# Attention in a four-layer graph network: scores turned so that the keys lie on the partitions, a multiplied mask instead of an added one, no maximum, and the old network kept behind a branch

## The chip, the cores and the metric

The kernel runs on one core of a Trainium2 chip. A core has five engines that work side by side: TensorE (PE; its loads of weights are listed as PEld), VectorE (DVE), ScalarE (ACT), GpSimd (POOL) and SyncE (SP, which issues transfers). The metric is the device time of one execution in microseconds, the median of several runs.

## The reference

There are 128 graphs of 64 nodes with 256 features. Four layers follow each other, each with a layer norm and a ReLU ahead of it and a residual sum after it. The change concerns the first two, which are attention layers with 8 heads of 32 features:

```python
# layer 0 (biases bq, bk, bv, bo)
scores = jnp.einsum('bhqd,bhkd->bhqk', q, k) / np.float32(np.sqrt(HD))
scores = jnp.where(adj[:, None, :, :] > 0, scores, jnp.float32(NEG))      # NEG = -9e15
attn = jax.nn.softmax(scores, axis=-1)
out = jnp.einsum('bhqk,bhkd->bhqd', attn, v)
return out.transpose(0, 2, 1, 3).reshape(b, n, D_OUT) @ Wo + bo
# layer 1 (only bo)
scores = jnp.einsum('bhqd,bhkd->bhqk', q, k) / math.sqrt(HEAD_DIM)
scores = scores + jnp.log(adjacency + 1e-06)[:, None, :, :]
attn = jax.nn.softmax(scores, axis=-1)
# ... the same as above
```

Layer 2 is a gated graph network of five steps (a product with the adjacency, then a GRU cell with two sets of 256x768 weights); layer 3 mixes a normalized graph convolution with a plain product by a gate. All is in fp32. Every node has an edge to itself, so no row of the adjacency is empty.

## The kernel before

Two graphs share the 128 partitions (a pair); four pairs make a group, and there are 16 groups. Python records every operation with an estimated cost, and a planner (`Plan.run`) then emits them in an order that mixes the attention of one group with the GRU of another and the last layer of a third. Small matmuls use parts of the array: the planner knows the modes T64 (tiles of 64x64: scores and aggregation), T32 (64 rows by 32 columns: the weighting of the values) and TURN (transpositions). PSUM is two sets of four banks, of which attention and the last layer share the tag "a" and the GRU's sums have the tag "g".

The attention of two pairs, one "step" (16 groups x 2 layers x 2 halves = 64 steps):

```python
# [cut: layer norm, projections q, k, v]
pss = [bank(f"s_{name}_{i}") for i in range(2)]

def scores():
    for i in range(2):                      # which graph of a pair
        for c in range(2):                  # which half of the heads
            for gp in range(2):             # which pair
                for rh in range(2):
                    # [cut: s, t0]
                    ps = pss[rh].tile.rearrange("p (h i k) -> p h i k", h=4, i=2)
                    nc.tensor.matmul(ps[gp * NODES : (gp + 1) * NODES, 2 * c : 2 * c + 2, i, :],
                                     qk[s, c, gp, 0, i * NODES : (i + 1) * NODES],
                                     k_exp[s, c, :, t0 : t0 + NODES], start=True, stop=True)
# [cut: the last step's weigh() is put ahead of scores(), its finish() behind]
for i in range(2):
    ps, e = pss[i], es[i]
    vec(dve(512), ... scalar_tensor_tensor(e, ps, scale, bias_at(pp) ..., op0=mult, op1=add))
    vec(dve(512), ... tensor_reduce(m, e8(), axis=X, op=max))
    vec2(dve(512), ... tensor_tensor(e8(), e8(), m ..., op=subtract))
    sca(act(512, 0.5), ... activation(e, e, AF.Exp))
    vec(dve(512), ... tensor_reduce(z, e8(), axis=X, op=add))
    vec(109, ... reciprocal(z, z))
    pool(1000, ... gpsimd.tensor_tensor(e8(), e8(), z ..., op=mult))
    pa = bank(f"aT_{name}_{i}")
    pe(437, turn, ...)                      # four 128x128 transpositions of e into pa
    sca(act(512), ... activation(aT, pa, AF.Copy))

po = [bank(f"o_{name}_{i}") for i in range(2)]

def weigh():
    for gp in range(2):
        s = slice(gp * NODES, (gp + 1) * NODES)
        for c in range(2):
            for q in range(4):
                for i in range(2):
                    rows, h = slice(i * NODES, (i + 1) * NODES), 4 * c + q
                    o = po[i][:, :D].rearrange("p (c t) -> p c t", c=2)
                    nc.tensor.matmul(o[q * HD : (q + 1) * HD, c, s], v[rows, gp, h * HD : (h + 1) * HD],
                                     aTs[q // 2][rows, 2 * c + q % 2, s], start=True, stop=True)

def finish():
    for i in range(2):
        vec(dve(256), ... tensor_copy(oT[:, i], po[i][:, :D] ...))
    # [cut: four 256-column matmuls of oT with w_o into py]
    vec(dve(512), ... tensor_tensor(xt, py, xt, op=add))
```

(Calls are shortened with "..."; the cost in front is the planner's, in ns.) For each group the mask is made ready once: `neg` is NEG where the adjacency is zero, on VectorE; `ladj = Ln(adj + 1e-6)` on ScalarE, once for two groups.

Of the kernel before, what the change touches and what calls it, by code (L numbers as in the profile page):

```python
# [11 lines left out]
ALU = mybir.AluOpType  # L12
# [62 lines left out]
FUSE = -1.1  # L75
FUSE_SPAN = 0.25


# [190 lines left out]


@with_exitstack
def gnn_stack_kernel(ctx: ExitStack, tc: tile.TileContext, a: dict, out: bass.AP):
    nc = tc.nc
    x, adj, nodemask = a["x"], a["adj"], a["nodemask"]
    n_pairs = x.shape[0] // 2
# [94 lines left out]
    with plan.strand(-3.0, 0.1):  # L370


        few = new("few", [P, 7 + PAIRS], 1)

# [4 lines left out]
        fill(slice(1, 1 + PAIRS), 1, -0.5)  # L379
        parity, k_bias = PAIRS + 1, PAIRS + 3  # L380
        fill(slice(parity, parity + 2), 2, 0.0)
        for q in range(4):
            fill(slice(parity + q % 2, parity + q % 2 + 1), 2, 1.0, slice(q * HD, (q + 1) * HD))
        ident = new("ident", [P, P], 1)
        pool(600, lambda: make_identity(nc, ident.tile), [], [ident])
# [13 lines left out]
        def fill_rows():  # L399
            r0 = 0  # L400
            for name in ("L0_gnn_bq", "L0_gnn_bk", "L2_gnn_b_ih", "L2_gnn_b_hh", "L0_gnn_bv"):
                n = a[name].shape[0] // P
                nc.scalar.dma_start(rows.tile[r0 : r0 + n, :], a[name].rearrange("(r p) -> r p", p=P))
                r0 += n
            nc.scalar.dma_start(rows.tile[r0 : r0 + n_pairs, :],
                                nodemask.rearrange("(t a) n -> t (a n)", a=2))
# [6 lines left out]
        def load_first(layer, i):  # L413
            t, j = (first[layer], i) if i < 2 else (first[2], layer)
            dma(256, lambda: nc.sync.dma_start(
                t[:, j], a[f"L{layer}_gnn_W{'qkv'[i]}"].rearrange("(c p) o -> p c o", p=P)), [], [(t, j)])
            return t, j
# [48 lines left out]
    with plan.strand(-0.9, 0.1):  # L466

        w_o, bo = attn[0]
        bvb = new("aT", [P, 4, P], 2, "bvb")
        pbo = bank("bvo")  # L470
        for c in range(2):
            vec(200, lambda c=c: nc.vector.tensor_copy(
                bvb[:, c, :], cols[:, 16 + c : 17 + c].to_broadcast([P, P])), [cols], [(bvb, c)])
            pe(mm(256), lambda c=c, w_o=w_o: nc.tensor.matmul(
                pbo[:, :D], bvb[:, c, :], w_o[:, c, :], start=c == 0, stop=c == 1),
                [(bvb, c), w_o], [pbo])
        vec(dve(256), lambda bo=bo: nc.vector.tensor_tensor(bo.tile, pbo[:, :D], bo.tile, op=ALU.add),
            [pbo, bo], [bo])
# [25 lines left out]
    def power(dst, src, at, eps, n, name):  # L504

        s = new("pw", [P, n], 3, f"pw_{name}")
        vec2(70, lambda: nc.vector.tensor_scalar(s.tile, at(), eps, None, op0=ALU.add), [src], [s])  # L507
        pool(660 if n == 2 else 970, lambda: nc.gpsimd.tensor_tensor(dst.tile, s.tile, few[:, 1 : 1 + n], op=ALU.pow),  # L508
             [s, (few, 1)], [dst], port=2)
# [24 lines left out]

    def norm_relu_t(xt, half, dst, access, writes, name, by_token=None, by_graph=False):

        st = new("st", [P, 2, 6], 3, f"st_{name}")
        mv = new("mv", [P, 2, 2], 3, f"mv_{name}")
        rstd = new("rstd", [P, 2], 3, f"rstd_{name}")
        for i in range(2):  # L540
            p = 2 * half + i
            vec(332, lambda p=p, i=i: nc.vector.bn_stats(st[:, i, :], xt[:, p, :]), [(xt, p)], [(st, i)])
            vec(83, lambda i=i: nc.vector.bn_aggr(mv[:, i, :], st[:, i, :]), [(st, i)], [(mv, i)])
        power(rstd, mv, lambda: mv[:, :, 1], EPS, 2, name)
        xn = new("xn", [P, 2, D], 1, f"xn_{name}")
        for i in range(2):
            p = 2 * half + i
            vec2(325, lambda p=p, i=i: nc.vector.tensor_scalar(
                xn[:, i, :], xt[:, p, :], mv[:, i, 0:1], rstd[:, i : i + 1],
                op0=ALU.subtract, op1=ALU.mult), [(xt, p), mv, rstd], [(xn, i)])  # L550
        if by_token is not None:
            sca(act(512), lambda: nc.scalar.activation(
                by_token[:, 2 * half : 2 * half + 2, :], xn.tile, AF.Relu), [xn], [(by_token, half)])
        transposed(dst, access, xn, lambda i: xn[:, i % 2, (i // 2) * P : (i // 2 + 1) * P],
                   f"lnT_{name}", True, writes, relu=True, by_graph=by_graph)
# [48 lines left out]
    def attend(layer, xt, half, bias, bias_at, name, plain):  # L604
# [131 lines left out]
# [5 lines that stand above are left out]
                            s = slice(rh * 2 * HD, (rh + 1) * 2 * HD)  # L741
                            t0 = (2 * gp + i) * NODES
                            ps = pss[rh].tile.rearrange("p (h i k) -> p h i k", h=4, i=2)
                            nc.tensor.matmul(ps[gp * NODES : (gp + 1) * NODES, 2 * c : 2 * c + 2, i, :],  # L744
                                             qk[s, c, gp, 0, i * NODES : (i + 1) * NODES],
                                             k_exp[s, c, :, t0 : t0 + NODES],
                                             start=True, stop=True)

        es = [new("e", [P, 4, 2 * NODES], 3, f"e_{name}_{i}") for i in range(2)]
        if waiting:  # L750
            _, weigh_last, reads, po_last, oT_last, finish_last = waiting.pop()
            pe(655, weigh_last, reads, po_last, holds=[oT_last], mode=T32)
            pe(860, scores, [qk, k_exp], pss, holds=es, mode=T64)
# [6 lines left out]

        aTs = []
        shape = [P, HEADS, NODES]
        for i in range(2):
            ps, e = pss[i], es[i]
            m = new("smax", [P, HEADS], 3, f"smax_{name}_{i}")
            z = new("ssum", [P, HEADS], 3, f"ssum_{name}_{i}")
# [30 lines left out]
# [6 lines that stand above are left out]
# [3 lines left out]
                                             v[rows, gp, h * HD : (h + 1) * HD],  # L806
                                             aTs[q // 2][rows, 2 * c + q % 2, s], start=True, stop=True)

        oT = new("oT", [P, 2, 2, P], 1, f"oT_{name}")

        def finish():
            for i in range(2):
                vec(dve(256), lambda i=i: nc.vector.tensor_copy(
                    oT[:, i], po[i][:, :D].rearrange("p (c t) -> p c t", c=2)), [po[i]], [(oT, i)])
            py = bank(f"y_{name}")
            for i in range(2):
                for c in range(2):
                    pe(mm(256), lambda i=i, c=c: nc.tensor.matmul(  # L818
                        py[:, i * D : (i + 1) * D], oT[:, i, c, :], w_o[:, c, :],
                        start=c == 0, stop=c == 1), [(oT, i), w_o], [py])  # L820
            vec(dve(512), lambda: nc.vector.tensor_tensor(
                xt[:, pp : pp + 2, :], py.tile.rearrange("p (t d) -> p t d", t=2), xt[:, pp : pp + 2, :],
                op=ALU.add), [py, (xt, pp), (xt, pp + 1)], [(xt, pp), (xt, pp + 1)])

        waiting.append((xt, weigh, [v, *aTs], po, oT, finish))

    def flush(xt):
# [3 lines left out]
        _, weigh, reads, po, oT, finish = waiting.pop()  # L831
        pe(655, weigh, reads, po, holds=[oT], mode=T32)
        finish()
# [320 lines left out]
    def front(g):  # L1154

        if g % ADJ_GROUPS == 0 and (g // ADJ_GROUPS + 1) * ADJ_GROUPS < n_groups:
# [4 lines left out]
        first = (g % ADJ_GROUPS) * PAIRS  # L1161
        neg = new("neg", [P, PAIRS, NODES], 1, f"neg_{g}")
        vec2(200, lambda: nc.vector.tensor_scalar(
            neg.tile, adjq[:, sel, :], 0.0, NEG, op0=ALU.is_le, op1=ALU.mult), [adjq], [neg])
        for layer in range(2):
            if layer and not g % ADJ_GROUPS:
                log_adj(g // ADJ_GROUPS)
            ladj = adj_vals[g // ADJ_GROUPS][1]
            for half in range(2):
                bias = ladj if layer else neg  # L1170
                bias_at = (lambda p, t=ladj, n=first: t.tile.rearrange("p t k -> p (t k)")[:, (n + p) * NODES : (n + p + 2) * NODES]) if layer else (
# [16 lines left out]
        norm = new("norm", [P, PAIRS], 5, f"norm_{g}")  # L1188
        power(norm, deg, lambda: deg.tile, 1e-6, PAIRS, f"deg_{g}")
        adjT = new("adjT", [P, PAIRS, P], 4, f"adjT_{g}")  # L1190
# [14 lines left out]
    def entry(g, xt):  # L1205
# [3 lines left out]
        for half in range(2):  # L1209
            norm_relu_t(xt, half, h, lambda half=half: h[:, :, half * HALF : (half + 1) * HALF],  # L1210
                        [(h, (0, half)), (h, (1, half))], f"{g}_2_{half}", ht)
        return h, ht
# [161 lines left out]
    for at, g, l in events:  # L1374
# [19 lines left out]
        if l + 1 == LAYERS:  # L1394
            with plan.strand(begin[g] + 2 + BACK + (BACK_LAST if g + 2 == n_groups else BACK_END if last else 0), BACK_SPAN):
                back(g, *held.pop(g))
    plan.run()

# [32 lines left out]
```

## Time and profile before

| | |
|---|---|
| time, median of 3 runs | 2527.14 us (2523.44 to 2527.82) |
| span of the profiled run | 2523.7 us |
| operations of one attention step | busy time of one, x number in the whole kernel |
| transposition of e (L786, PE) | 273 ns, x512 |
| weighting (L805, PE) | 224 ns a record, x4096 |
| scores with mask to e (L767, DVE) | 670 and 684 ns, x128 in all |
| maximum, subtraction, sum (L772, L774, L777, DVE) | 671, 688, 672 ns, x128 each |
| reciprocal of 8 sums (L779, DVE) | 192 ns (median), x128 |
| exp (L776, ACT) | 630 ns, x128 |
| e by the reciprocal sum (L780, POOL) | 1175 ns, x128 |
| copy of aT (L790, ACT) | 589 ns, x128 |
| copy of o (L813, DVE) | 414 ns, x128 |

How to read the views. The page gives the busy time of each engine and its share of the span. The busy time of TensorE counts overlapping records: an fp32 matmul leaves two records, and the next starts before the last is over, so the time between starts is what a matmul costs. The chain of work that ended last is followed back from the last instruction: it lists what each moment of the span was waiting for, with the time until the next piece starts. The stretches give the busy time of every engine in windows of the span. The waits say which engine sat idle until whom. "L786" is line 786 of the kernel.

### The profile page before, as it was taken

To read this page: it belongs to the slowest core of one execution; us is meant where nothing else is said; L and a number is where in the kernel's file an instruction comes from. 1 tells how busy PE (TensorE), PEld (TensorE's weight loads), DVE (VectorE), ACT (ScalarE), POOL (GpSimd) and SP (SyncE) were. 2 spreads that over 40 slices of the span, in tenths; PEclk is the share of its full clock that TensorE was granted. 3 is DMA by queue.
4 is the path that set the end of the run, shared out by engine and by line. 5 is a ranking of instruction groups with operands and counts; after the bars stand their busy time and mean duration, and the time that the engine had idled before them with its cause. 6 is when DMAs were issued, how large, how long until landed. Compare 5 with 4: busy or idle time off the path is not lost.

```text
span 2523.7 us, 58158 instructions
## 1 busy us (share of the span) xinstructions
PE 2501.1 (99%) x23511; PEld 2150.9 (85%) x23511; DVE 2038.7 (81%) x4632; ACT 1394.8 (55%) x2806; POOL 879.7 (35%) x892
## 2 busy tenths in 40 slices
PE   9999999999999999999999999999999999999998
PEld 7788888888888888888888888888888888888885
DVE  7886787887878888798877978878788887887667
ACT  4456555555556555565555655556555555555444
POOL 5632323424333333333423334243333333333121
PEclk9999999999999999999999999999999999999999
DMA  6511212113121122222113121131211222211120
GB/s 198 174 67 61 93 49 79 62 54 106 51 99 64 61 75 71 79 71 73 59 68 101 50 84 65 52 101 52 98 64 64 68 71 79 71 49 67 49 71 18
DMA packets 78256, 188.47 MB, mean 75 GB/s; under 512 B 14802, under 2 KB 66852, under 8 KB 67108
## 3 DMA queue, kind: packets, MB, share of 16 engines
q1 hardware_dynamic: 77872, 184.71, 21.8%
q8 instruction: 186, 3.05, 0.5%
q14 instruction: 82, 0.67, 0.1%
q10 hardware_dynamic: 116, 0.04, 0.0%
HBM read 166.70 MB, written 18.02 MB: 73 GB/s over the span
## 4 chain that ended last, share of the span: by engine, by line
PE 96%; DVE 3%; ACT 0%; issue 0%; POOL 0%; DMA 0%; DVEq 0%; POOLq 0%; ACTq 0%
PE gb L932 22%; PE gc L932 17%; PE nb L932 11%; PE nc L932 8%; PE qkvb L682 6%; PE qkvc L682 5%; PE y L818 4%; PE agg L972 3%; PE l3b L1254 3%; PE s L744 3%; PE lnT L522 2%; PE l3c L1254 2%; PE aT L786 2%; PE hT L522 2%; PE o L805 2%; PE hom L1321 1%
## 5 line engine op out<-in xcount | busy, mean ns | idle before, releaser
L1041 POOL TENSOR_TENSOR sn<-h,sn 128x512 f32<-128x512 f32 x158 | 209.1, 1327 | 464.1 <-ACT sn L1039 463.7
L508 POOL TENSOR_TENSOR rstd<-pw,few 128x2 f32<-128x2 f32 x128 | 101.6, 794 | 482.9 <-DVE pw L507 459.7
L780 POOL TENSOR_TENSOR e<-e,ssum 128x512 f32<-128x512 f32 x128 | 149.4, 1175 | 315.9 <-DVE ssum L779 284.5
L932 PE MATMUL gb<-Th,w_hh 128*128 128x256 f32 x960 | 248.1, 381 | 0.0
L932 PE MATMUL gb<-Ta,gv 128*128 128x256 f32 x960 | 246.5, 379 | 0.0
L901 POOL TENSOR_TENSOR Th<-h 128x256 f32<-128x256 f32 x160 | 129.5, 829 | 249.6 <-PE nb L932 177.0
L932 PEld LDWEIGHTS gb<-Th,w_hh 128*128 128x128 f32 x960 | 178.1, 190 | 28.6 <-POOL Th L901 0.4
L932 PEld LDWEIGHTS gb<-Ta,gv 128*128 128x128 f32 x960 | 179.6, 190 | 25.3
L1039 ACT ACTIVATE sn<-sn,b_n 128x512 f32<-128x512 f32 x158 | 114.2, 724 | 123.4 <-DVE sn L1037 121.6
L932 PE MATMUL gc<-h,w_hh 128*128 128x256 f32 x640 | 166.1, 382 | 0.1
L932 PE MATMUL gc<-agg,gv 128*128 128x256 f32 x640 | 165.6, 381 | 0.0
L1043 DVE SCALAR_TENSOR_TENSOR sn<-sg,sn 128x512 f32<-128x512 f32 x158 | 107.4, 686 | 58.5 <-POOL sn L1041 58.3
L1024 ACT ACTIVATE sg<-sg,b_rz 128x512 f32<-128x512 f32 x158 | 105.5, 714 | 78.5 <-DVE sg L1004 78.5
L932 PE MATMUL nb<-Th,w_hh 128*128 128x256 f32 x480 | 144.1, 382 | 0.0
L932 PE MATMUL nb<-Ta,gv 128*128 128x256 f32 x480 | 143.0, 380 | 0.0
L901 POOL TENSOR_TENSOR Th<-h,Th 128x256 f32<-128x256 f32 x160 | 139.1, 869 | 10.4 <-DVE h L1045 4.6
L818 PE MATMUL y<-w_L_gnn_Wo,oT 128*128 128x256 f32 x512 | 138.9, 382 | 0.0
L1035 DVE SCALAR_TENSOR_TENSOR sn<-sg,sn 128x512 f32<-128x512 f32 x158 | 110.4, 700 | 34.8 <-ACT sn L1146 31.7
L985 DVE TENSOR_TENSOR Ta<-agg 128x256 f32<-128x256 f32 x160 | 92.3, 588 | 51.5 <-PE nb L932 41.2
L932 PEld LDWEIGHTS gc<-agg,gv 128*128 128x128 f32 x640 | 118.4, 190 | 16.9 <-issue 2.5
L996 ACT ACTIVATE p5g<-gc 128x512 f32<-128x512 f32 x79 | 46.9, 594 | 149.5 <-PE gc L932 149.4
L932 PEld LDWEIGHTS gc<-h,w_hh 128*128 128x128 f32 x640 | 116.3, 190 | 15.5 <-ACT sg L1031 0.5
(224 smaller groups left out, 6943.4 us busy)
## 6 DMA issues: line engine op xcount, KB each, us to landing
gv<-gates SPq DMA_DIRECT2D x80, 1344.0 KB, 6.0
qw<-kept SPq DMA_DIRECT2D x203, 192.0 KB, 2.4
x<-in_x_dram SPq DMA_DIRECT2D x32, 256.0 KB, 5.5
out_dram<-x SPq DMA_DIRECT2D x32, 256.0 KB, 2.3
gates<-gv SPq DMA_DIRECT2D x5, 1344.0 KB, 5.3
adjq<-in_adj_dram SPq DMA_DIRECT2D x8, 256.0 KB, 4.2
gw<-in_L_gnn_weight_dram SPq DMA_DIRECT2D x5, 256.0 KB, 6.4
kept<-s SPq DMA_DIRECT2D x8, 128.0 KB, 3.5
```

What stands on the lines that cost most here:

```text
L508: pool(660 if n == 2 else 970, lambda: nc.gpsimd.tensor_tensor(dst.tile, s.tile, few[:, 1 : 1 + n], op=ALU.pow), [s, (few, 1)], [dst], port=2)
L682: nc.tensor.matmul(bk[:, j * P : (j + 1) * P], lhs, rhs, start=first and j == 0, stop=True, skip_group_check=True)
L780: pool(1000, lambda e8=e8, z=z: nc.gpsimd.tensor_tensor(e8(), e8(), z[:, :, None].to_broadcast(shape), op=ALU.mult), [e, z], [e])
L818: pe(mm(256), lambda i=i, c=c: nc.tensor.matmul(py[:, i * D : (i + 1) * D], oT[:, i, c, :], w_o[:, c, :], start=c == 0, stop=c == 1), [(oT ...
L901: pool(690, lambda: nc.gpsimd.tensor_tensor(T[:, i, :], x(), y(), op=ALU.subtract), reads, [(T, i)])
L932: nc.tensor.matmul(bank_[:, col * HALF : (col + 1) * HALF], at(g, n), rhs(), start=first and j == 0, stop=True, skip_group_check=True)
L1024: sca(act(TOK, 1.5), lambda k=k, col=col: nc.scalar.activation(g_v[:, :, k, :], g_v[:, :, k, :], AF.Tanh, bias=b_rz[:, col : col + 1], sca ...
L1035: vec2(dve(TOK), lambda: nc.vector.scalar_tensor_tensor(a_(), r(), 1.0, a_(), op0=ALU.add, op1=ALU.mult), [*ts[0], n_v], [n_v])
L1039: sca(act(TOK, 1.5), lambda: nc.scalar.activation(a_(), a_(), AF.Tanh, bias=b_n[:, oc : oc + 1]), [n_v, b_n], [n_v])
L1041: pool(1230, lambda: nc.gpsimd.tensor_tensor(b_(), hh(), a_(), op=ALU.subtract), [*hp, n_v], [n_v])
L1043: vec2(dve(TOK), lambda: nc.vector.scalar_tensor_tensor(b_(), z(), 1.0, b_(), op0=ALU.add, op1=ALU.mult), [*ts[1], n_v], [n_v])
L1254: pe(mm(384), lambda: nc.tensor.matmul(bk[:, : 3 * P], b(), w3[:, :, n, :], start=first, stop=True, skip_group_check=True), [w3, *reads], ...
```

## The change

It is made so that the softmax needs fewer passes. The roles of keys and queries are exchanged in the projections, so the scores come out with the keys on the partitions, which is how the weighting needs them: the transposition and its copy fall away. Without a maximum, exp is applied to the scores right out of PSUM, and the mask is multiplied in afterwards (for layer 0 it is adj > 0, for layer 1 adj + 1e-6, since exp(s + log a) = a exp(s)), so it has to be turned as well, once a group on TensorE. A sum over keys is now a sum over partitions: a matmul with a block of equal constants gives it, spread over the 32 rows of each head, and the division is done after the weighting. Powers of two keep the numbers in range. Since a softmax without a maximum can overflow, the means of the last layer norm are gathered, a flag says whether all are finite, and if not, the whole network is computed again the old way behind a branch.

```diff
+WEIGH = (655, 1100)
+MASK_UP = 2.0 ** 32
+SUM_DOWN = 2.0 ** -42
+WEIGH_UP = 2.0 ** 52
+Y_DOWN = 2.0 ** -94
...
+def gnn_stack_kernel(tc: tile.TileContext, a: dict, out: bass.AP):
+    nc = tc.nc
+    with tc.tile_pool(name="flag", bufs=1) as keep:
+        flag = keep.tile([P, 1], mybir.dt.int32, name="flag")
+        network(tc, a, out, flag)
+        beyond = nc.values_load(flag[0:1, 0:1])
+        with tc.If(beyond > 0, preferred_fallthrough_block=False):
+            network(tc, a, out, None)
...
+    lean = flag is not None
+    order_qkv = "kqv" if lean else "qkv"
...
-                            nc.tensor.matmul(ps[gp * NODES : (gp + 1) * NODES, 2 * c : 2 * c + 2, i, :],
+                            to, at = (i, gp) if lean else (gp, i)
+                            nc.tensor.matmul(ps[to * NODES : (to + 1) * NODES, 2 * c : 2 * c + 2, at, :],
...
-        es = [new("e", [P, 4, 2 * NODES], 3, f"e_{name}_{i}") for i in range(2)]
+        es = [new("e", [P, 4, 2 * NODES], 4 if lean else 3, f"e_{name}_{i}") for i in range(2)]
...
-            pe(655, weigh_last, reads, po_last, holds=[oT_last], mode=T32)
+            pe(WEIGH[lean], weigh_last, reads, po_last, holds=[oT_last], mode=T32)
...
+            if lean:
+                sca(act(512, 0.5), lambda ps=ps, e=e: nc.scalar.activation(
+                    e.tile, ps.tile.rearrange("p (h k) -> p h k", h=4), AF.Exp, scale=scale), [ps], [e])
+                pool(1000, lambda e=e: nc.gpsimd.tensor_tensor(
+                    e.tile, e.tile, bias_at(pp)[:, None, :].to_broadcast([P, 4, 2 * NODES]), op=ALU.mult),
+                    [e, bias], [e])
+                continue
...
+            for q in range(4):
+                for i in range(2):
+                    rows = slice(i * NODES, (i + 1) * NODES)
+                    nc.tensor.matmul(po[i][q * HD : (q + 1) * HD, D:], ones[rows, :],
+                                     aTs[q // 2].tile.rearrange("p (c r) t -> p r c t", c=2)[rows, q % 2],
+                                     start=True, stop=True)
...
+        def divide(i):
+            rz = new("rz", [P, D], 2, f"rz_{name}_{i}")
+            vec(dve(256) + 40, lambda: nc.vector.reciprocal(rz.tile, po[i][:, D:]), [po[i]], [rz])
+            vec(dve(256), lambda: nc.vector.scalar_tensor_tensor(
+                oT[:, i].rearrange("p c t -> p (c t)"), rz.tile, WEIGH_UP, po[i][:, :D], op0=ALU.mult, op1=ALU.mult),
+                [po[i], rz], [(oT, i)])
...
+            masks = [new(f"mask{layer}", [P, PAIRS, NODES], 2, f"mask{layer}_{g}") for layer in range(2)]
+            ps_m = bank(f"mask_{g}")
+            # [two transpositions of adj into ps_m]
+            pe(220, turn_adj, [adjq, ident], [ps_m], holds=masks, mode=TURN)
+            for layer, (by, op) in enumerate(((0.0, ALU.is_gt), (1e-6, ALU.add))):
+                vec(dve(256), lambda ...: nc.vector.tensor_scalar(masks[layer] ..., ps_m[:, : 2 * P], by, MASK_UP,
+                    op0=op, op1=ALU.mult), [ps_m], [masks[layer]])
...
+    if lean:
+        with plan.strand(n_groups + 0.2, 0.1):
+            # [means of the last layer norm times zero, summed, compared with zero: 1 where finite]
+            pe(120, lambda: nc.tensor.matmul(
+                count[:1, :1], once[:, n + 1 : n + 2], few[:, parity_sum : parity_sum + 1], start=True, stop=True), ...)
+            vec(70, lambda: nc.vector.tensor_scalar(
+                flag[0:1, 0:1], count[:1, :1], float(P), None, op0=ALU.not_equal), [count], [])
```

Cuts are marked with "..." and brackets. The final residual sum multiplies by `Y_DOWN` on the way, in the same instruction as before with one more factor; the layer norm ahead of layer 2 writes its means into the tile `sure`; the second network, behind the branch, is the kernel before.

## The prediction

> **What bounds the kernel now.** I read the page's busy table first, then its slices and its chain, then the chain again in order of time around one attention step, then busy time by stretches, and last the queue of waits of TensorE.
>
> ```profile
> span 2523.7 us, 58158 instructions
> PE 2501.1 (99%) x23511; PEld 2150.9 (85%) x23511; DVE 2038.7 (81%) x4632; ACT 1394.8 (55%) x2806; POOL 879.7 (35%) x892
> PE 96%; DVE 3%; ACT 0%; issue 0%; POOL 0%; DMA 0%; DVEq 0%; POOLq 0%; ACTq 0%
> ```
>
> TensorE is busy 99% and 96% of the chain that ended last is its own work; VectorE's 81% is a second load, not a bound. So the first question is what the change does to TensorE's own sum. The page's groups give means of overlapping records (a 256-column matmul "lasts" 381 ns), so I take costs from the chain in time, where each piece ends when the next begins:
>
> ```profile
> 82 pieces in order of time: start us, us, what
> ...
> 1011.40 0.86 PE gc L932 x4
> 1012.26 0.79 PE o L805 x53
> 1013.05 1.05 PE s L744 x32
> 1014.10 1.06 PE gc L932 x4
> 1015.16 0.43 PE y L818 x2
> ...
> 1028.54 0.44 PE aT L786 x4
> ...
> 1030.28 0.44 PE aT L786 x4
> 1030.71 0.44 PE adjT L1195 x4
> ```
>
> Read here: one 256-column fp32 matmul leaves two records and takes 0.43 us (y, x2); four transpositions take 0.435 us on average; the weighting of the values (o, 64 records of 32 matmuls) 0.79 us, the scores (s) 1.05 us. The matmul after the small ones (gc, 1.06 against 0.86) pays for the way back. By stretches (span, then busy PE, PEld, DVE, ACT, POOL, clock, DMA share, GB/s):
>
> ```profile
> 0.00:30.00 30.00, 27.64 (x242) 22.25 (x243) 16.83 (x48) 13.96 (x24) 10.24 (x24) 1.00 0.89 276
> 30.00:60.00 30.00, 27.18 (x284) 20.73 (x286) 29.17 (x65) 16.11 (x26) 21.80 (x22) 1.00 0.29 100
> 60.00:120.00 60.00, 57.66 (x647) 45.75 (x640) 52.12 (x135) 28.00 (x60) 36.13 (x40) 1.00 0.53 182
> 1000.00:2000.00 1000.00, 1000.00 (x9604) 870.80 (x9603) 820.35 (x1895) 563.19 (x1144) 349.68 (x345) 1.00 0.22 74
> 2500.00:2523.70 23.70, 14.95 (x45) 8.51 (x44) 15.15 (x42) 10.19 (x23) 3.60 (x5) 0.82 0.10 34
> ```
>
> In the middle TensorE has no idle time that another engine could give back. Idle time lies in the first 120 us (2.36 + 2.82 + 2.34 = 7.5 us; from 30 to 60 us VectorE is the full one, 29.17 of 30) and in the last 24 us, where no attention runs. The wait that the change removes is small:
>
> ```profile
> PE aT L786 <- POOL e L780: 1.7, 1, 1.7
> ```
>
> **What the skill says.** (1) The Trainium skill, "TensorEngine Tiling (Array Packing)", Key Properties: tiles of the array run independently, and a change of tiling mode drains the array. The trace agrees with both: 16 score matmuls of two passes at 0.107 us a pass (half of the 0.213 that 256 columns stream) would take 3.4 us one by one and take 1.05; and the passage back shows as 1.06 instead of 0.86 us. (2) "TensorE: Matmul & The Clock Gate", Measured speedup vs the span model: a pack of tiles lasts one matmul plus about 4 ns for each further tile. For eight tiles of 0.43 us that is an estimate of 0.46 us. The trace has no pack of eight with 256 columns, but in the weighting's first 0.25 us eight new records start every 56 ns, about the 53 ns that 64 columns stream, so eight tiles do run at full rate there. (3) "VectorE: DVE Perf Modes", First, the fixed hardware budget: the reciprocal is an iterated division with a repeat count of 8. The trace has it only for 8 columns, 192 ns at the median, and can't tell a fixed extra from one for each column. (4) "Runtime: NRT & Kernel Launch", Instruction fetch mechanics: a taken branch to a far place waits for its instructions to be fetched. No branch of that kind is in this trace.
>
> **The change part by part, on TensorE.** There are 64 attention steps (16 groups, 2 layers, 2 halves).
> - Removed: 8 transpositions of e a step, 2 x 0.435 us, x64 = 55.7 us.
> - Added: 8 matmuls of a constant [64, 32] by 256 columns a step, each on its own tile (2 row halves by 4 column quarters). If all eight run side by side: 0.43 us plus the issue of seven more. The planner's constant goes from 655 to 1100 ns, 0.445 us, in keeping with this. x64 = 28.5 us.
> - Added: 2 transpositions of adj a group, 16 x 2 x 0.109 = 3.5 us, and one 1x1 matmul at the end, 0.2 us.
> - Moved: scores and weighting are as many as before, only keys and queries change sides. The planner's new order of instructions makes 151 visits to the small tilings instead of 140. From the starts of the matmuls in the trace, a visit with all that it delays costs 1.29 us for an aggregation alone, 0.99 for a weighting alone, 1.23 for scores alone, 2.02 for weighting and scores together, 2.16 for scores and aggregation, and 0.05 less if a transposition follows. The old order sums to 228.5 us, the new one (64 aggregations alone, 20 weightings, 10 scores, 41 weighting and scores, 16 other pairs; 49 followed by a transposition) to 229.3. +0.8 us.
> Sum on TensorE: -55.7 + 28.5 + 3.5 + 0.2 + 0.8 = -22.7 us.
>
> **Beside TensorE.** VectorE loses, for each of the 128 score tiles, the biased copy (677 ns), two reductions (671 and 672), the subtraction (688) and the small reciprocal (192): 2.90 us, 371 us in all. It gains a reciprocal of 256 columns from PSUM (about 0.45 us if one column a cycle, taken from the 414 ns copy of that size plus the small fixed extra), 58 us, and two mask passes a group, about 12 us; the product that replaces the copy of o costs about the same. VectorE falls by some 300 us to about 1740, 70%. ScalarE loses 128 copies of 589 ns (75 us), the 8 logarithms and the table loads around them. GpSimd has the same multiplication, now by the mask. Almost nothing of this is on the path, since the middle of the kernel has no idle TensorE. What I do give for it: of the 7.5 us at the start I take back 3 (the wait there ran through the softmax on VectorE), of the scattered waits 1.
>
> **The end.** Behind the last product every engine loads the flag, compares, and leaves the not-taken side by a branch over the whole second network. In the trace the last store is issued at 2520.5 and the span ends at 2523.7, with 1.6 us of waiting for that store, so a part of the loads and branches is covered, the last far jump is not. I choose +3 us, of 1 to 7.
>
> Total: 2527.1 - 22.7 - 3 - 1 + 3 = 2503.4, rounded to 2503 us, 0.95% less.
>
> **The rivals.**
> - Four tiles at a time. Should the eight long streams share two lanes per row half, the sums cost 0.86 us a step instead of 0.445, 27 us more, and the change is worth nothing: about 2530. For it: no pack of eight long streams is in the trace, and over its whole length the weighting is much slower than 56 ns for eight (0.79 us for 64 records); against it: the starts in its first 0.25 us, and the planner's 1100. One in ten.
> - VectorE was the hidden bound. If 81% and the many stalls by its queue cost TensorE time, 300 us off it would bring far more than 4 us: 2480 or less. Against it: 1000.00 busy in the 1000 us of the middle; a gap shorter than a matmul's own latency hides there, but the starts of the matmuls leave only some 10 us of such gaps from 120 to 2300 us.
> - A slow reciprocal. At about 5 cycles a column (the 8-column one would allow that) it takes 1.4 us instead of 0.45, twice between weighting and output product, and holds two of the four PSUM banks longer. VectorE would still come to about 1860 us, below before; I expect 0 to 8 us of it on TensorE, through waits of y for oT and of scores for a bank.
> - The branch is taken, and all is done twice: about 5000 us. The flag counts 128 partitions whose means are finite, and nothing in inputs of this size overflows. One in a hundred.
>
> **Range and chances.** The terms for the sums (0.43 to 0.50 us a step, 4 us), for the start and the new order (5 us either way), the tail (1 to 7) and a spread of 4 us in the runs before give 2491 to 2516. Faster by over 2% needs 50 us, which TensorE's sum does not contain: 0.04. Slower by over 2%: only a taken branch, or long waits for the divided values: 0.03. Within 2%: 0.93.
>
> **What would show it.** The sums: pieces "o" of the chain at about 1.2 us instead of 0.79, and no aT. TensorE still at 99%, its busy time down by 20 to 26 us; at 0.8 us more a step the first rival holds. VectorE near 1740 us, and the mean of the reciprocal tells 0.45 from 1.4 us; y waiting for oT would show its harm. The stretches 30 to 120 us should have 3 us less idle TensorE, and the time from the last store's issue to the end should grow from 3.2 to about 6 us. I am wrong if the middle shows idle TensorE, or if the gain there exceeds the sum above.

## The result, and the profile after

The changed kernel takes 2650.6 us (median; 2646.6 to 2652.5), the kernel before 2527.1 on the same chip: ratio 1.0489, 95% interval 1.0474 to 1.0504. It is 123.5 us slower, not 24 us faster.

From the page of the kernel after, the busy table and the chain by engine:

```profile
span 2650.6 us, 58506 instructions
PE 2544.9 (96%) x24057; PEld 2142.7 (81%) x24057; DVE 1994.2 (75%) x4140; ACT 1300.2 (49%) x2654; POOL 872.7 (33%) x894
PE 83%; DVE 13%; ACT 3%; issue 1%; POOL 0%; DMA 0%; DVEq 0%; ACTq 0%; POOLq 0%
```

VectorE is less busy than before (1994 us against 2039, 75% against 81%), and yet it now holds 13% of the chain where it held 3%. TensorE has fallen from 99% to 96%, and that is in the middle of the kernel too, where it had been full (stretch; span, busy PE, PEld, DVE, ACT, POOL, clock, DMA share, GB/s):

```profile
1000.00:2000.00 1000.00, 972.71 (x9379) 824.44 (x9379) 778.86 (x1645) 509.51 (x1053) 326.47 (x328) 1.00 0.21 69
```

What put VectorE into the chain is one new operation. All instructions on the tile `rz` in the kernel after (minimum, median, maximum in ns), and who waited for what it feeds:

```profile
L858 DVE RECIPROCAL rz<-o x128: 1689/1752/1759, 31.9 to 2392.1; 128x256 f32<-128x256 f32 x128
L859 DVE SCALAR_TENSOR_TENSOR oT<-rz,o x128: 356/407/422, 35.2 to 2394.0; 128x256 f32<-128x256 f32 x128
...
who waited for it (us, times):
  PE y L873: 29.9, 19
  PE hom L1400: 9.6, 12
```

The reciprocal of 256 columns takes 1.75 us, not the 0.45 of the prediction or the 375 ns that the planner was given. The chain in time shows what that does (start, length, piece):

```profile
1088.28 0.72 PE o L842 x49
1089.06 0.54 PE o L850 x14
1089.60 1.74 DVE rz L858
1091.34 0.28 DVE Ta L1041
1091.69 0.17 issue
1091.86 1.75 DVE rz L858
1093.61 0.61 DVE Ta L1041 x2
1094.22 0.66 DVE sn L1063
...
1096.89 0.34 DVE qk L730
1097.23 0.21 DVE v L732
1097.48 0.94 PE qkvc L711 x6
```

Two reciprocals stand in VectorE's queue ahead of Ta, sn, qk and v, none of which needs them. VectorE works off its queue in the order in which the planner emitted it: its 4140 instructions start in exactly the same sequence here and in e1 below, where a short copy stands for each reciprocal. From 1089.6 to 1097.5 the chain is VectorE alone, and the next TensorE work on it, a projection (qkvc) of another group, waits for v. TensorE has other work for most of these 7.9 us and stands idle for 1.8 of them, so VectorE's 13% of the chain is not the loss itself. The waits are spread over many victims, and the list of TensorE's waits in the kernel after names the result of the division only in part:

```profile
PE y L873 <- DVE oT L859: 29.9, 19, 2.3
PE nc L988 <- DVE sn L1063: 15.0, 12, 1.2
PE hom L1400 <- DVE oT L859: 9.6, 12, 0.8
PE qkvc L711 <- DVE v L732: 8.4, 14, 1.3
```

The end grew as well. The last store is issued at 2642.91 us, 7.7 us ahead of the end of the span; before, 3.2 us.

```profile
2642.91 0.37 SPq L1425 DMA_DIRECT2D out_dram<-x  x1
```

### The profile page after: what moved, and what is told of

It is laid out like the page before. It is cut to its first block, busy times and chain, and to the rows that moved or that the text cites. A ratio compares the mean times of both kernels' runs of the same rounds, so it can differ in the third digit from the quotient of the medians.

```text
span 2650.6 us, 58506 instructions
## 1 busy us (share of the span) xinstructions
PE 2544.9 (96%) x24057; PEld 2142.7 (81%) x24057; DVE 1994.2 (75%) x4140; ACT 1300.2 (49%) x2654; POOL 872.7 (33%) x894
## 4 chain that ended last, share of the span: by engine, by line
PE 83%; DVE 13%; ACT 3%; issue 1%; POOL 0%; DMA 0%; DVEq 0%; ACTq 0%; POOLq 0%
PE gb L988 20%; PE gc L988 13%; PE nb L988 9%; DVE rz L858 7%; PE nc L988 7%; PE qkvb L711 5%; PE y L873 4%; PE qkvc L711 4%; PE agg L1028 3%; PE l3b L1333 3%; PE l3c L1333 2%; PE hT L547 2%; PE lnT L547 2%; PE s L774 1%; PE o L842 1%; PE hom L1400 1%
## 5 line engine op out<-in xcount | busy, mean ns | idle before, releaser
L1097 POOL TENSOR_TENSOR sn<-h,sn 128x512 f32<-128x512 f32 x158 | 203.7, 1293 | 631.5 <-ACT sn L1095 631.5
L798 POOL TENSOR_TENSOR e<-e,mask 128x512 f32<-128x512 f32 x128 | 167.0, 1325 | 315.0 <-ACT e L796 315.0
L858 DVE RECIPROCAL rz<-o 128x256 f32<-128x256 f32 x128 | 219.5, 1738 | 55.0 <-PE o L850 55.0
L957 POOL TENSOR_TENSOR Th<-h 128x256 f32<-128x256 f32 x160 | 122.6, 786 | 325.2 <-PE nb L988 214.8
L873 PE MATMUL y<-w_L_gnn_Wo,oT 128*128 128x256 f32 x512 | 140.4, 389 | 31.5 <-DVE oT L859 29.9
L1091 DVE SCALAR_TENSOR_TENSOR sn<-sg,sn 128x512 f32<-128x512 f32 x158 | 116.1, 741 | 37.4 <-ACT sn L1202 32.7
L873 PEld LDWEIGHTS y<-w_L_gnn_Wo,oT 128*128 128x128 f32 x512 | 96.7, 193 | 54.0 <-issue 35.1
```

Source lines behind the costliest of these rows:

```text
L798: pool(1000, lambda e=e: nc.gpsimd.tensor_tensor(e.tile, e.tile, bias_at(pp)[:, None, :].to_broadcast([P, 4, 2 * NODES]), op=ALU.mult), [e ...
L858: vec(dve(256) + 40, lambda: nc.vector.reciprocal(rz.tile, po[i][:, D:]), [po[i]], [rz])
L873: pe(mm(256), lambda i=i, c=c: nc.tensor.matmul(py[:, i * D : (i + 1) * D], oT[:, i, c, :], w_o[:, c, :], start=c == 0, stop=c == 1), [(oT ...
L957: pool(690, lambda: nc.gpsimd.tensor_tensor(T[:, i, :], x(), y(), op=ALU.subtract), reads, [(T, i)])
L1091: vec2(dve(TOK), lambda: nc.vector.scalar_tensor_tensor(a_(), r(), 1.0, a_(), op0=ALU.add, op1=ALU.mult), [*ts[0], n_v], [n_v])
L1097: pool(1230, lambda: nc.gpsimd.tensor_tensor(b_(), hh(), a_(), op=ALU.subtract), [*hp, n_v], [n_v])
```

## The experiments

The theory had two parts. A1: the reciprocal is longer than the planner knows, so it stands in the wrong place of VectorE's queue and TensorE waits behind it. A2: the score matmuls became slower, because the change swapped which loop picks the column tile, so that neighbouring matmuls now stand on fewer different tiles. The main rival B: the new order of instructions, or the new small matmuls, cost the time, with VectorE only 75% busy.

**e1_copy: a copy instead of the reciprocal**

```diff
-vec(dve(256) + 40, lambda: nc.vector.reciprocal(rz.tile, po[i][:, D:]), [po[i]], [rz])
+vec(dve(256) + 40, lambda: nc.vector.tensor_copy(rz.tile, po[i][:, D:]), [po[i]], [rz])
```

> The reciprocal of 256 columns (1.74 us measured) becomes a copy of the same columns, under the same planner cost, so the order of instructions stays; the result leaves out the division. Theory A, the long reciprocal stands in VectorE's queue and TensorE waits behind it: the reciprocal should cost some 110 us, so 2535 to 2550 us, with the copy near 0.41 us and VectorE near 1825 us busy. Rival B, the new order and the slower small matmuls are what costs, VectorE being only 75% busy: over 2620 us.

Measured: 2538.6 us, ratio to before 1.0056 (1.0040 to 1.0073). The sequence of instructions is the same on every engine, one operation of 0.42 us stands where one of 1.75 stood, and 112 us of the 123.5 are gone. TensorE is back at 99%; the busy table and the chain:

```profile
PE 2512.2 (99%) x24057; PEld 2142.0 (84%) x24057; DVE 1837.7 (72%) x4140; ACT 1300.7 (51%) x2654; POOL 875.5 (35%) x894
PE 98%; DVE 1%; ACT 1%; issue 0%; DMA 0%; POOL 0%; DVEq 0%; ACTq 0%; POOLq 0%
```

Rival B, which wanted over 2620, falls.

**e2_loops and e3_both: the score loops in the other order, without and with the copy**

```diff
-            for i in range(2):
-                for c in range(2):
-                    for gp in range(2):
+            for c in range(2):
+                for gp in range(2):
+                    for i in range(2):
                         for rh in range(2):
```

> Only the loops of the score matmuls change places: graph i moves inside c and gp, so that four matmuls in a row stand on four different tiles again, as in the kernel before. Theory A: each block of scores loses 0.49 us, 64 of them 31 us, so 2615 to 2625 us, and a block of scores alone costs 1.23 us again instead of 1.72. Rival B, the array works off queued tiles in any order and the scores lengthen for another reason (the other side's operands, or the drain behind the longer weighting): no change, 2645 to 2655 us.

> Copy in place of the reciprocal and the loops in the other order, together; leaves out the division. Theory A (two causes, and nothing else large): what was predicted for the change itself, 2500 to 2515 us. If a third cause is in it (the mask, the planner's order, the sums), 2525 us or more stay.

Measured: e2 2653.9 us (ratio 1.0512, 1.0494 to 1.0529), no gain over the change; e3 2514.2 us (0.9954, 0.9937 to 0.9971), 24 us less than e1. The chains in time of e1 and of e3, the same place in the program, show that the scores did get faster:

```profile
1093.41 0.50 PE o L850 x14
1093.91 1.52 PE s L774 x32
1095.43 0.63 PE nb L988 x2
```

```profile
1081.15 0.50 PE o L850 x14
1081.65 1.03 PE s L774 x32
1082.68 0.63 PE nb L988 x2
```

The first is e1, 1.52 us for the scores; the second e3, 1.03 us, as in the kernel before (1.05). From the starts of the matmuls, a visit for scores alone costs 1.72 us in the change and in e1, and 1.23 in the kernel before, in e2 and in e3. So A2 is right about TensorE, and my expectation of e2 was wrong about the time. The time is the one that rival B of e2 named, but its reason, scores that stay slow, is not what the trace shows: in e2 TensorE has by the starts 64 x 0.49 = 31 us less work (its busy sum falls from 2544.9 to 2521.5) and waits that much longer. The stretch of e2:

```profile
1000.00:2000.00 1000.00, 962.53 (x9368) 812.69 (x9366) 777.78 (x1639) 508.25 (x1052) 327.24 (x327) 1.00 0.21 69
```

Busy PE is down by 10 us in 1000 and the time is the same: as long as the queue of VectorE sets the pace, TensorE's work is not what counts.

**e4_told and e5_told_loops: the planner is told what the reciprocal lasts**

```diff
-vec(dve(256) + 40, lambda: nc.vector.reciprocal(rz.tile, po[i][:, D:]), [po[i]], [rz])
+vec(1690, lambda: nc.vector.reciprocal(rz.tile, po[i][:, D:]), [po[i]], [rz])
```

> The reciprocal stays, but the planner is told 1690 ns for it instead of 375, so it can place other work around it. If the harm is the misjudged place in VectorE's queue, most of it comes back: 2560 to 2590 us. If it is the reciprocal's length itself (latency between weighting and output product, banks held), little: 2625 us or more.

> The planner is told 1690 ns for the reciprocal and the score loops are in the other order; the result is whole. Theory A, now with the two causes in a row (the misjudged reciprocal makes VectorE's queue the bound, which hid the longer scores; with TensorE the bound again, the loops count): 31 us off the 2549.7 of the told kernel, 2517 to 2527. Rival B, the loops matter only where the reciprocal is gone: 2540 to 2552.

Measured: e4 2549.7 us (1.0098, 1.0081 to 1.0115); e5, which has the loops too, 2521.2 us (0.9985, 0.9978 to 0.9991). One number in the planner gives back 101 us with every operation in place; e4 came out better than I had expected. The order that results differs in most places of VectorE's queue, so e4 alone can't tell the true length from a luckier order; its list has no wait of a TensorE matmul for the divided values any more, where the kernel after has 29.9 us of y alone. e5 then takes another 28.5 us: with TensorE the bound again, the loops count. It is whole, including the branch, and is the first version that beats the kernel before, by 0.15%. The chain of e4, and the busy table of e5:

```profile
PE 97%; DVE 1%; ACT 1%; issue 0%; POOL 0%; DMA 0%; DVEq 0%; ACTq 0%; POOLq 0%
```

```profile
PE 2485.1 (99%) x24057; PEld 2113.9 (84%) x24057; DVE 1978.1 (79%) x4140; ACT 1309.6 (52%) x2654; POOL 898.2 (36%) x894
```

VectorE does the same 128 reciprocals of 1.74 us and is as busy as in the change (1978 us against 1994); only their place in the queue differs.

**e6_half: the reciprocal on half of the columns**

```diff
-vec(dve(256) + 40, lambda: nc.vector.reciprocal(rz.tile, po[i][:, D:]), [po[i]], [rz])
+vec(dve(256) + 40, lambda: (nc.vector.tensor_copy(rz[:, : D // 2], po[i][:, D : D + D // 2]),
+                            nc.vector.reciprocal(rz[:, D // 2 :], po[i][:, D + D // 2 :])), [po[i]], [rz])
```

> The kernel after the change, with the reciprocal on 128 of the 256 columns and a copy on the other 128, under the old planner cost; leaves out half of the division. If the reciprocal costs by the column (about 6.5 ns), this one lasts 0.9 to 1.0 us; if it is a fixed extra, 1.6 us or more. Time: if waits grow in proportion to what the planner does not know (0.7 of 1.3 us), some 2590 to 2605 us; if slack swallows the first part, under 2575.

Measured: 2576.2 us (1.0204, 1.0188 to 1.0220), between the two expectations, 1 us above the second. The instructions on `rz` in e6:

```profile
L858 DVE COPY rz<-o x128: 220/283/293, 32.0 to 2320.2; 128x128 f32<-128x128 f32 x128
L859 DVE RECIPROCAL rz<-o x128: 933/946/948, 32.2 to 2320.3; 128x128 f32<-128x128 f32 x128
```

946 ns for 128 columns, 1744 to 1752 for 256 and 192 for 8 (in the kernel before, and there not from PSUM) lie on one line of 6.3 ns a column: it costs by the column. The harm does not grow in proportion: copy and half reciprocal last 0.81 us longer than e1's copy, the whole reciprocal 1.33, and the harm is 38 us against 112. Part of the unplanned time finds slack.

**e8_no_branch: the flag is computed, but nothing is loaded and there is no branch and no second network**

```diff
-        beyond = nc.values_load(flag[0:1, 0:1])
-        with tc.If(beyond > 0, preferred_fallthrough_block=False):
-            network(tc, a, out, None)
```

> As the told kernel with the other loops, but the loads of the flag, the branch and the second network are left out (the flag is still computed). Theory: the branch costs only behind the last store, 7.7 us from its issue to the end in the trace of the change against 3.2 before, so 4.5 us less than the kernel with the branch. Rival, a program of twice the length also costs while it runs: 8 us less or more.

Measured: 2518.2 us (0.9969, 0.9957 to 0.9980), 3 us less than e5 by the medians, 4 by the ratios. That is about what the tail shows (4.5 us), so these runs show no cost of the second network while the kernel runs. This one leaves out the fallback, so it is not a replacement.

**e9_split and e10_all_told: other planning around the same work**

In e9 each reciprocal of e5 is two instructions of 128 columns, planned at 855 ns each. The diff of e9, and of e10, which tells two more costs:

```diff
-            vec(1690, lambda: nc.vector.reciprocal(rz.tile, po[i][:, D:]), [po[i]], [rz])
+            for c in range(2):
+                vec(855, lambda c=c: nc.vector.reciprocal(
+                    rz[:, c * P : (c + 1) * P], po[i][:, D + c * P : D + (c + 1) * P]), [po[i]], [(rz, c)])
```

```diff
-WEIGH = (655, 1100)
+WEIGH = (655, 1150)
...
-                pool(1000, lambda e=e: nc.gpsimd.tensor_tensor(
+                pool(1200, lambda e=e: nc.gpsimd.tensor_tensor(
                     e.tile, e.tile, bias_at(pp) ...
```

> As the told kernel with the other loops, but each reciprocal in two instructions of 128 columns with 855 ns each, so that the planner can put something between. If what is left of the reciprocal is that it blocks VectorE's queue for 1.7 us at a time, 3 to 8 us less than the kernel with whole reciprocals; if it is only its sum on VectorE, the same within 2 us or a little more (128 more instructions).

> As the told kernel with the other loops, and the planner is also told 1200 ns for the multiplication by the mask (1000 before; 1.25 us measured from start to start) and 1150 for the weighting with its sums (1100 before; 1.48 us measured for the whole visit against 0.99 without the sums). Theory, the planner's knowledge is what keeps TensorE fed: 2510 to 2520, at or below the 2521.2 of that kernel. Rival, the order depends on small numbers by chance: anywhere from 2510 to 2565.

Measured: e9 2562.3 us (1.0146, 1.0130 to 1.0161), e10 2535.5 us (1.0036, 1.0022 to 1.0050). e9 missed its expectation; e10 missed that of the theory and lies in the range of its rival, an order that hangs on small numbers. e9 was to show whether 1.7 us in one piece is what hurts, and it is 41 us slower than e5; the wait of TensorE that stands out in e9 is

```profile
PE qkvc L711 <- DVE v L732: 30.2, 12, 2.5
```

2.5 us in each of 12 groups, at one place where the new order puts VectorE's work for v late. e5's list has no such line. A part of the 41 us is not waiting but a slower TensorE: the mean granted clock is 0.990 in e9 and 0.998 in e5, by my estimate 0.008 x 2560 = at most some 20 us (e12 below shows where it comes from). So e9 says nothing of the split as such; it says, with e10, that the order drawn up from slightly other costs can be 14 or 41 us worse by itself. Why the planner lands there I did not follow further, and 1690 ns is not shown to be the best number.

**e11_told_copy: e5's order, with a copy where the reciprocal stood**

```diff
-vec(1690, lambda: nc.vector.reciprocal(rz.tile, po[i][:, D:]), [po[i]], [rz])
+vec(1690, lambda: nc.vector.tensor_copy(rz.tile, po[i][:, D:]), [po[i]], [rz])
```

> The order of instructions of the told kernel with the other loops, but a copy runs where the reciprocal stood (the planner still believes 1690 ns); leaves out the division. It says what the reciprocal still costs when it is planned for. If its length is hidden beside TensorE: 2514 to 2521, at most 7 us less. If it still holds TensorE up: under 2510.

Measured: 2520.3 us (0.9973, 0.9964 to 0.9983), by the ratios 3 us less than e5. Planned for, 128 reciprocals of 1.74 us cost some 3 us of time; unplanned, 112.

**e12_before_rz: the same surprise in the kernel before**

```diff
-                vec(dve(256), lambda i=i: nc.vector.tensor_copy(
-                    oT[:, i], po[i][:, :D].rearrange("p (c t) -> p c t", c=2)), [po[i]], [(oT, i)])
+                vec(dve(256), lambda i=i: (nc.vector.reciprocal(
+                    oT[:, i], po[i][:, :D].rearrange("p (c t) -> p c t", c=2)), nc.vector.tensor_copy(
+                    oT[:, i], po[i][:, :D].rearrange("p (c t) -> p c t", c=2))), [po[i]], [(oT, i)])
```

> The kernel before, with a reciprocal of the same 256 columns of o ahead of each copy to oT, which overwrites it; the planner does not know of it, so the order is the old one, and the result stays whole. It asks whether a step of 1.7 us on VectorE that the planner doesn't know costs about 100 us there too. VectorE goes from 2039 to about 2260 us busy. Theory (waiting in VectorE's queue): 2600 us or more. Rival (the harm is peculiar to the new order): 2530 to 2560.

Measured: 2789.4 us (1.1039, 1.1021 to 1.1057), 262 us more than the kernel before. Its busy table, its chain and its longest waits of TensorE:

```profile
PE 2588.2 (93%) x23511; PEld 2186.8 (78%) x23511; DVE 2258.4 (81%) x4760; ACT 1395.9 (50%) x2806; POOL 880.6 (32%) x892
PE 72%; DVE 25%; issue 1%; POOL 1%; ACT 1%; DMA 0%; DVEq 0%; ACTq 0%; POOLq 0%
```

```profile
PE y L819 <- DVE oT L814: 52.9, 54, 1.5
PE gb L933 <- DVE sg L1005: 35.2, 13, 2.9
PE lnT L522 <- DVE oT L814: 30.6, 15, 3.0
```

The same picture without anything of the change: VectorE is no busier by share than before (81%), and TensorE waits for oT and for sums of the GRU that stand behind the surprise. The harm is not peculiar to the new order. That it is more than twice the 112 us has three candidates. The surprise is larger, 1.75 us each time against 1.33; VectorE is fuller (2258 us of work against 1994), which I did not test alone; and TensorE's clock is lower behind long waits. Of the 264 us between the two profiled spans, idle TensorE makes up 177, and the same 23511 records are busy for 87 us more. The mean granted clock is 0.976 in e12 and 0.998 before. One wait of 2.9 us for sg, and what follows it (busy PE first; the clock is the third number from the end):

```profile
1000.00:1004.00 4.00, 1.28 (x4) 1.05 (x5) 2.55 (x4) 0.91 (x2) 1.25 (x2) 0.90 0.29 66
1004.00:1008.00 4.00, 4.00 (x16) 3.41 (x15) 0.00 (x0) 0.89 (x2) 1.05 (x2) 0.67 0.00 0
```

In the second stretch the clock is 0.67, and a matmul of y takes 0.85 us from start to start instead of 0.43. In e9, 9 of the 12 waits of 2.5 us have such a stretch of half the clock (3.4 us) at or behind them; e1 and e5, without a wait over 1.5 us, have none before 2470 us. By the mean clocks this is worth an estimated 0.022 x 2788 = 61 us of the 262 in e12, at most. In the change it is less: 0.994 against 0.998 in e1, some 11 us of the 112. So an unplanned step costs its wait and, where the wait is long, slower matmuls too.

## Why the prediction was wrong

- **What bounds the kernel: right for the kernel before, and carried over wrongly.** TensorE was the bound, and e3 and e5 are bound by it too (99%). The changed kernel isn't. I had asked only whether VectorE's sum grows; what counted was whether its queue delivers at the time for which the order was made.
- **The sums on TensorE: right in kind.** 0.445 us a step was expected; from the starts of the matmuls a visit for weighting alone went from 0.99 to 1.48 us, 0.50 us a step and 32 us in all instead of 28.5. The first rival (four tiles at a time, 0.86 us) fell: eight long streams do run side by side.
- **"Moved: scores and weighting are as many as before": a term missed.** As many, but slower by 0.49 us a step, 31 us in all. The diff showed it: `to` was `gp`, an inner loop, and became `i`, the outermost, so eight matmuls in a row stay on two tiles. With this TensorE's own sum is not -22.7 but -55.7 + 32 + 3.7 + 0.8 + 31 = +12 us; e1, with the order of the change and no long reciprocal, has a busy sum of 2512 us against 2501 before.
- **"Beside TensorE": the step that failed.** It concluded "Almost nothing of this is on the path, since the middle of the kernel has no idle TensorE"; the runs show 27 us of idle TensorE in the 1000 us of the middle, and 112 us of harm. The reciprocal was put at 0.45 us, with the planner's 375 ns as a hint; it measures 1.75. The rival "A slow reciprocal" named the mechanism, waits of y for oT, with 1.4 us and "0 to 8 us" on TensorE. The length was near, the effect wrong by more than ten times: 112 us (e1). I took VectorE's free quarter to be able to absorb it, and it can, at about 3 us (e11 against e5), but only where the order of the queue was made with the true length (e4: 101 us back). VectorE's own sum was off too, 1994 us against 1740: some 157 of it is the long reciprocal (e1: 1838), and the rest is mostly that the prediction took whole durations off a busy sum that counts overlaps once. From before to e1 the durations fall by 269 us, the busy sum by 201.
- **The rival "VectorE was the hidden bound"** failed as I put it: with 194 us less work on VectorE (e3: 1845 us) TensorE has no less idle time in its middle than before. The lesson of e12 is the other side of it: the order was so tight that an unplanned 1.7 us a time shows at once.
- **The end: +3 us was near.** The tail grew by 4.5 us, and e8 gives 3 to 4.
- **The sum, with both causes out.** 2525.3 (before, beside e3) - 55.7 + 32 + 3.7 + 0.8 + 4.5 = 2510.6 us; e3 measures 2514.2. The 3 us that I took back at the start show there (idle TensorE in the first 120 us 4.4 us against 7.5), so e3 lies some 7 us above what the terms give; that gap is not traced. The change, well planned and with the loops mended, is worth 4 us (e5), not 24: of the 20 us between, 3.5 are the sums, 1.5 the tail, some 7 the order and the reciprocal (e5 against e3), and the rest is the untraced gap and the 1 us of scattered waits.

## What to carry to other kernels

An in-order engine with a quarter of its time free can still stop another that is full: ask of a new operation not only what it adds to a sum but what stands behind it in its queue, and whether whoever fixed the order knew its length. A cost in a planner is a claim, and it may be measured for one operation and guessed for the next; check it against a trace of that operation at that size before trusting an order built on it. When loops around tiled matmuls change which index picks the tile, look at the tiles of neighbouring matmuls, and mend the bound first: in e2 a true saving of 31 us on TensorE was worth nothing until VectorE's queue was in order.

## What the runs showed of the hardware

- The reciprocal on VectorE costs about 6.3 ns a column in fp32: 192 ns for 8, 946 for 128 (895 in e9), 1744 to 1752 for 256, where a copy of 256 from the same place takes 418. The Trainium skill, "VectorE: DVE Perf Modes", First, the fixed hardware budget, tells of an iterated division with a repeat count of 8 and gives no time; by the runs I estimate some six VectorE cycles a column (6.3 ns at the 0.96 GHz of Specifications, same page).
- The order of matmuls over tiles matters: 16 score matmuls took 1.03 us with four tiles in turn and 1.52 with two in turn for eight matmuls. With matmuls on four tiles next to each other in the program, more of their work ran side by side.
- Eight matmuls of 64 rows by 32 columns with 256 columns each, one on each tile, added 0.50 us behind the weighting; one alone over the whole array takes 0.43.
- Leaving out the second network by a branch lengthened the time from the last store's issue to the end by 4.5 us (7.7 against 3.2); e8 without it is 3 to 4 us faster. "Runtime: NRT & Kernel Launch", Instruction fetch mechanics, says that a branch taken to a far place waits for its instructions to be fetched; the longer tail agrees with it, but no run here shows the fetch itself.
- A wait of TensorE can cost more than itself. Behind a wait of 2.9 us in e12 the granted clock was 0.67 over 4 us, and a 256-column matmul took 0.85 us instead of 0.43; the mean clock of the whole run was 0.976, against 0.998 in the kernel before.
